# Layer 3 of a fused four-layer kernel: gate chain in a PSUM tile of its own, five padded images, block copies moved from DMA to ScalarE and GpSimd

## The chip, the cores and the metric

The kernel runs on one core of one Trainium2 chip. Its time is the device time of one execution in microseconds. The core has five engines that matter here: TensorE (PE, with its weight loads PEld), VectorE (DVE), ScalarE (ACT), GpSimd (POOL) and SyncE (SP), whose queue starts the DMAs.

## The reference

Four layers work one after the other on x of shape (4, 256, 48, 48), each on a group-normalised input and each added to x: attention with eight heads, an 11-tap gated block, non-local attention with batch norm, and layer 3, which alone the change touches (with the few lines ahead of it):

```python
xw = _gn(x)                                   # group norm, 32 groups
p = jnp.mean(xw, axis=(2, 3))
h = jax.nn.leaky_relu(p @ attn_w1.T, 0.01)    # 256 -> 64
a = jax.nn.sigmoid(h @ attn_w2.T)             # 64 -> 256
y = xw * a[:, :, None, None]
y = depthwise_conv3x3(y, refine_w, 'SAME') + refine_b
y = (y - mean_hw(y)) * rsqrt(var_hw(y) + 1e-5)
x = x + leaky_relu(y, 0.01)
```

So layer 3 gates each channel with a number that a small two-layer network makes of the channels' means (the gate chain), convolves each channel with its own 3x3 filter, and normalises each channel of each image.

## The kernel before

Channels lie on the 128 partitions, in two halves (NK = 2); an image has 2304 pixels in a row. Layer 3 works on eight tiles: four images (order 1, 2, 3, 0) times two halves. For each tile the following is done.

- **Product and grow.** `w_product` (L1444) multiplies the last step of layer 2 into PSUM, `grow` (L1497, VectorE) scales it, adds x and writes it into a padded image of 50 by 50 (`pads`, tile i uses `pads[i % 4]`). Three products and three grows make a tile; they share one PSUM buffer, `w_tile()`. `border` (L1506, L1509, GpSimd) writes the rim. `square` (L1521, ScalarE) takes the sum of squares of each third.
- **Spread.** TensorE does the depthwise convolution with small weights, 32 channels at a time, that read three column-shifted copies of the channels on different partitions. `spread_out` fills these copies (`shifted`, three buffers of half an image): eight blocks that change partition go by DMA, four that stay on their partitions by GpSimd (first half), or two by DMA and two by ScalarE (second half). `place` issues one block (L1535 to L1541).
- **Convolution.** `Conv.products` (L1662) makes one sixth of the tile in PSUM (`cv_tile()`, three buffers, each holding two sixths): 12 matmuls, which the profile shows as 24 records.
- **Statistics and end.** `evict` (L1674, ScalarE) writes each third to SBUF with its sum, `centre` (L1681) makes a rough mean of the first third, the other `square` (L1685, ScalarE) takes the squares about it, `moments`, `scales` and `shift` (L1693 to L1733, VectorE, with a root on GpSimd, L179) give scale and offset, `scale` (L1739, ScalarE) applies them, `leak` (L1745) and `gain` (L1750) on VectorE apply the leaky ReLU and add x, `store` (L1756) starts the DMA to the output. The last tile takes its statistics with `bn_stats` (L1705) from PSUM.
- **Gate chain.** For each image once, `Chain.steps`: `total` (L1580), `groups` (L1587, a matmul), `inverse` (L1591 and a root on GpSimd), `pooled`, `first_layer` (L1602), `hidden` (L1610), `second_layer` (L1615), `gate` (L1622, ScalarE) and `scaled` (L1626 to L1631). Its matmuls write columns 384 and up of the convolution's PSUM tile in use (`now["ps"]`), and ScalarE reads them out (`read`, L1575). `judge` (L1768 to L1782) takes one vote on the range of earlier sums in the same manner.

The order on every engine is fixed by hand: a list of events, each with a slot and a rank. A slot is the time of one convolution sixth, six to a tile, 48 in all (T). Within a slot the ranks run FRONT, CONV, PRODUCT, GROW, MID, EVICT, SMALL, MOMENTS, SQUARE, SCALE, LAST, PLACE, STORE, and the instructions go into the engines' queues in that order (strict order on all five). `put_tile`, `put_before` and `put_chain` say in which slot each step falls, t being the tile's first slot:

```python
at(t - 11 + c, PRODUCT, lambda c=c: product(c))
at(max(0, t - 6 + 3 * h), PLACE, lambda i=i, h=h: spread_out(i, h))
at(t + 10 + g, LAST, lambda g=g: cv.leak(g))
put_chain(max(t - 1, 0), chains[i // NK].steps(8 if i else 7))
```

Ahead of the first slot stands a stretch that ends layer 2: the last unit of attention is summed (`total_here`, L399 and L401), folded (L387), divided (L391), multiplied for the batch statistics (L1084, L1365, L1136), `note` (L407 to L410) records sums for the vote, and batch scale and offset follow (L1374 to L1387). Then the first two tiles are grown (L1497), spread by `spread_first` and squared.

Of the kernel before, what the change touches and what calls it, by code (L numbers as in the profile page):

```python
# [78 lines left out]
def usual_path(  # L79
# [315 lines left out]
    def total_here(u):  # L395

        ps = pj_tile()
        for h, c in enumerate(HALVES):
            nc.tensor.matmul(ps[c, :SL], lhsT=ones, rhs=u["acc"][:, h, :], start=True, stop=True)  # L399
        u["rinv"] = rpool.tile([P, SL], F32, tag="rinv", name="rinv")  # L400
        nc.vector.reciprocal(u["rinv"], ps[:, :SL])  # L401
        u["l"] = ps
# [24 lines left out]
    def last(u, t):  # L427

        take(u)
        if u.get("soon"):  # L430
            todo = [
                (fills, 1, lambda: total_here(u)), (due, 2, lambda: fold(u, nc.vector)),
                (due, 2, lambda: divide(u, nc.vector)),
            ]
            if u.get("final"):
                noted.append(lambda: note(u))
            else:
                todo.append((due, 2, lambda: note(u)))
# [920 lines left out]
    attend(phases)  # L1359
    for b in range(NX):  # L1360
        sample_means(b)
    last_y = [w_mul(B - 1, k, L2C - 1, wide=True) for k in range(NK)]
    for k in range(NK):
# [23 lines left out]
    nc.vector.tensor_sub(bi2, vec[:, V_WB, :], bi2)  # L1387
    noted[0]()
    strict.close()
# [37 lines left out]
    CL = CH - 2  # L1427
    pads = [lp.tile([P, W2 * W2], F32, tag=f"pad{i}", name=f"pad{i}") for i in range(4)]
    shifted = [lp.tile([P, 4, CH], F32, tag=f"sh{i}", name=f"sh{i}") for i in range(3)]

    def rows_of(i):
        return pads[i % 4].rearrange("p (r c) -> p r c", c=W2)

# [18 lines left out]
    first = [w_product(0, c, cv_tile()) for c in range(L2C)]  # L1452
    ahead = [w_product(1, 0, w_tile())]

# [14 lines left out]
    def columns_of(ps, n):  # L1469
# [4 lines left out]
        of_groups, lhsT=gmat, rhs=means.rearrange("p b k -> p (b k)"), start=True, stop=True  # L1474
    )
    gm = lp.tile([P, B, NK], F32, name="gm")
    edge = lp.tile([P, B, NK], F32, name="edge")
# [52 lines left out]
    def place(i, h, j, q, how):  # L1530
        to = shifted[(2 * i + h) % 3][32 * q : 32 * q + 32, j, :CL]
        c0 = h * HB * W2 + SHIFT[j, q]
        fr = pads[i % 4][32 * j : 32 * j + 32, c0 : c0 + CL]
        if how == "sp":
            nc.sync.dma_start(to, fr)  # L1535
        elif how == "act":
            nc.scalar.copy(to, fr)
        elif how == "pool":
            nc.gpsimd.tensor_copy(to, fr)
        else:  # L1540
            nc.vector.tensor_copy(to, fr)  # L1541
# [3 lines left out]
    def spread_out(i, h):  # L1545

        for j, q in AWAY:
            place(i, h, j, q, "sp")
        for j in range(4):
            place(i, h, j, j, ("sp", "act")[j % 2] if h else "pool")  # L1550

# [11 lines left out]
    class Chain:  # L1563
# [4 lines left out]

        def steps(self, last):
            of, b = {}, self.b  # L1570

            def read(p):
                of["raw"] = small.tile([P, NK], F32, tag="chain", name="chain")
                n = 1 if p < P else NK
                nc.scalar.copy(of["raw"][0:p, 0:n], of["ps"])  # L1575
                return of["raw"][0:p, 0:n]

# [7 lines left out]
            def groups():  # L1585
                of["ps"] = now["ps"][:, 0:NK]
                nc.tensor.matmul(of["ps"], lhsT=gmat, rhs=of["sq"], start=True, stop=True)  # L1587

            def inverse():
                gv = small.tile([P, NK], F32, tag="gn_gv", name="gn_gv")  # L1590
                nc.vector.tensor_scalar(gv, of["raw"], GN_EPS, None, ALU.add)  # L1591
                of["rs"] = small.tile([P, NK], F32, tag="gn_rs", name="gn_rs", bufs=6)
                rsqrt(of["rs"], gv)
# [5 lines left out]
            def first_layer():  # L1599
                of["ps"] = now["ps"][0:D, 0:1]  # L1600
                for k in range(NK):
                    nc.tensor.matmul(  # L1602
                        of["ps"], lhsT=w1[:, k, :], rhs=of["pm"][:, k : k + 1],
                        start=k == 0, stop=k == NK - 1,
                    )

            def hidden():
                raw = of["raw"][0:D, 0:1]
                of["hl"] = hl = small.tile([D, 1], F32, tag="hl", name="hl")
                nc.vector.scalar_tensor_tensor(hl, raw, SLOPE, raw, ALU.mult, ALU.max)  # L1610

            def second_layer():
                of["ps"] = now["ps"][:, 0:NK]
                for k in range(NK):
                    nc.tensor.matmul(  # L1615
                        of["ps"][:, k : k + 1], lhsT=w2[:, k * P : (k + 1) * P], rhs=of["hl"],
                        start=True, stop=True,
                    )
# [5 lines left out]
            def scaled():  # L1624
# [8 lines left out]
            return [  # L1633
                (0, MID, total), (1, SMALL, groups),
                (2, FRONT, lambda: read(P)), (2, MID, inverse),
                (3, MID, pooled), (4, SMALL, first_layer),
                (5, FRONT, lambda: read(D)), (5, MID, hidden), (last - 1, SMALL, second_layer),
                (last, FRONT, gate), (last, MID, scaled),
            ]

    class Conv:
# [9 lines left out]
        def products(self, s):  # L1651
            g, h = s // 2, s // L2C
            if s % 2 == 0:
                self.ps[g] = cv_tile()
            now["ps"] = self.ps[g][:, s % 2, SL:]
            out = self.ps[g][:, s % 2, :SL].rearrange("p (r c) -> p r c", c=HW)
# [105 lines left out]
    def judge():  # L1762
# [10 lines left out]
        def count():  # L1773
            of["ps"] = now["ps"][0:1, 0:1]
            nc.tensor.matmul(of["ps"], lhsT=of["okm"], rhs=ones[:, 0:1], start=True, stop=True)

        def read():
            of["n"] = lp.tile([1, 1], F32, name="votes")
            nc.scalar.copy(of["n"], of["ps"])

        def compare():
            nc.vector.tensor_scalar(sound, of["n"], P - 0.5, None, ALU.is_ge)  # L1782

        return [(0, FRONT, lows), (1, SMALL, count), (2, FRONT, read), (2, MID, compare)]

# [33 lines left out]

    now = {}  # L1820

    def put_chain(t, parts):
# [3 lines left out]
    def put_before(t, i):  # L1826
# [10 lines left out]
        at(t - 11, PLACE, lambda: border(i))  # L1837

    def put_tile(t, cv, final):
# [14 lines left out]
        for g in range(NG3):  # L1854
            at(t + 9 + (0 if soon else g), SCALE, lambda g=g: cv.scale(g))
            dt = 10 + (min(g, 1) if soon else g)
            at(t + dt, LAST, lambda g=g: cv.leak(g))
            at(t + dt, LAST, lambda g=g: cv.gain(g))
            at(t + dt + 1 - soon, STORE, lambda g=g: cv.store(g))

# [4 lines left out]
    for i, cv in enumerate(convs):  # L1865
# [12 lines left out]
    for t in range(max(T, max(events) + 1)):  # L1878
        for _, fn in sorted(events.get(t, ()), key=lambda job: job[0]):
            fn()  # L1880
        if t == T - 1:
            cv = convs[-1]
            cv.stats(NSL - 1)
            cv.aggregate()
            cv.scales()
            cv.shift()
            for g in range(NG3):
                cv.scale(g, cv.ps[g])
                cv.leak(g)
                cv.gain(g)  # L1890
                cv.store(g)
    said = nc.values_load(sound[0:1, 0:1])
# [845 lines left out]
```

## Time and profile before

| what | value |
|---|---|
| median of three runs | 3557.1 us (3553.09 to 3557.35) |
| the profiled execution | 3548.05 us |
| its span, first to last instruction | 3546.3 us |
| its mean granted TensorE clock | 0.990 |
| first convolution slot starts | 3375.0 us into the span |
| last convolution matmul ends | about 3528.1 us |
| last VectorE operation ends | about 3541.5 us |

Busy us of each engine in stretches of layer 3 (two tiles each in the first four rows, then the tail):

| stretch, us | PE | DVE | ACT | POOL | clock | DMA share |
|---|---|---|---|---|---|---|
| 3375.0 to 3414.75 | 36.3 | 12.1 | 26.3 | 19.0 | 0.87 | 0.78 |
| 3414.75 to 3456.5 | 34.6 | 30.9 | 28.4 | 18.0 | 0.88 | 0.77 |
| 3456.5 to 3497.3 | 33.8 | 27.5 | 28.1 | 16.7 | 0.92 | 0.89 |
| 3497.3 to 3528.1 | 26.7 | 18.8 | 21.0 | 7.4 | 0.94 | 0.63 |
| 3528.1 to 3546.3 | 0.0 | 11.6 | 2.8 | 0.5 | 0.60 | 0.35 |

Layer 3 with its lead-in is the last 190 us, about 5% of the span. A line of the timeline has start and length in us, the engine, the line of the kernel, output and input, the number of instructions that were merged, and in brackets the idle time before with what ended it.

### The profile page before, as it was taken

The numbers are of one execution on the slowest core, as the hardware profiler recorded it, in microseconds if no ns is written. First come the engines' busy times: TensorE is split into PE (matmuls) and PEld (weight loads), VectorE is DVE, ScalarE is ACT, GpSimd is POOL, SyncE is SP. The second block draws the span as 40 slices with busy tenths as digits, with TensorE's granted clock in tenths as the row PEclk, the third lists the DMA queues.
The fourth block names the chain that finished last, engine by engine and source line by source line (L and its number), as shares of the span: only waits on it lengthen the run. The fifth ranks groups of instructions, "written<-read, shape, count | busy, mean of one in ns | idle before, by whom it ended". The sixth has DMA issues, their size and how long they took to land. (4 is left out here: it accounts for less than half of the span.)

```text
span 3546.3 us, 88389 instructions
## 1 busy us (share of the span) xinstructions
PE 3431.1 (97%) x37036; PEld 1729.9 (49%) x37036; DVE 2547.1 (72%) x3475; ACT 2370.6 (67%) x3842; POOL 814.8 (23%) x619
## 2 busy tenths in 40 slices
PE   8999999999999999999999999999999999898886
PEld 4554555554444444444444444444444445565422
DVE  3455545567788788687887886878878879655856
ACT  4665666665886796558867976579668755565465
POOL 2333333321101010000111100110100117665442
PEclk9999999999999999999999999999999999999988
DMA  2211111111111111221111111111111100000076
GB/s 94 48 26 22 26 22 26 22 26 22 22 26 22 26 22 26 55 46 21 26 20 26 22 27 21 26 22 26 22 22 22 22 8 6 6 7 6 4 199 200
DMA packets 122423, 118.93 MB, mean 34 GB/s; under 512 B 59056, under 2 KB 112928, under 8 KB 121248
## 3 DMA queue, kind: packets, MB, share of 16 engines
q1 hardware_dynamic: 119264, 111.03, 16.7%
q8 instruction: 292, 4.78, 0.6%
q10 hardware_dynamic: 2752, 2.17, 0.2%
q14 instruction: 115, 0.94, 0.1%
HBM read 56.99 MB, written 11.80 MB: 19 GB/s over the span
## 5 line engine op out<-in xcount | busy, mean ns | idle before, releaser
L296 ACT ACTIVATE pt<-sc 128x768 f32<-128x768 f32 x1944 | 1475.3, 811 | 727.1 <-PE sc L290 717.0
L336 DVE TENSOR_TENSOR acc<-acc,pt 128x768 f32<-128x768 f32 x1368 | 1369.3, 1001 | 174.3 <-ACT pt L296 74.4
L310 PE MATMUL av<-pt,v 64*64 64x384 f32 x13824 | 1274.7, 484 | 0.0
L290 PE MATMUL sc<-q,k 64*64 64x384 f32 x13824 | 1269.9, 482 | 0.5 <-ACT pt L296 0.5
L290 PEld LDWEIGHTS sc<-q,k 64*64 64x64 f32 x13824 | 525.4, 133 | 589.5 <-issue 543.4
L310 PEld LDWEIGHTS av<-pt,v 64*64 64x64 f32 x13824 | 518.1, 133 | 598.9 <-issue 565.9
L391 POOL TENSOR_TENSOR o<-o,rinv 128x384 f32<-128x384 f32 x95 | 115.7, 1218 | 1735.8 <-DMA rinv<-rinv 1735.8
L321 POOL TENSOR_TENSOR half<-pt 128x768 f32<-128x768 f32 x189 | 364.4, 1932 | 537.9 <-ACT pt L296 499.9
L336 DVE TENSOR_TENSOR acc<-acc,half 128x768 f32<-128x768 f32 x171 | 194.1, 1135 | 229.5 <-POOL half L321 228.5
L674 DVE SCALAR_TENSOR_TENSOR x<-pj,bo,x 128x384 f32<-128x384 f32 x192 | 118.4, 617 | 311.2 <-PE pj L661 309.9
L850 ACT ACTIVATE prod<-pd,wt 128x256 f32<-128x256 f32 x486 | 337.1, 765 | 0.2
L578 PE MATMUL pj<-xs,w 128*128 128x384 f32 (+1 forms) x720 | 275.4, 505 | 0.0
L578 PEld LDWEIGHTS pj<-xs,w 128*128 128x128 f32 x720 | 124.1, 189 | 127.9 <-issue 39.5
L310 PE MATMUL av<-pt,qv 64*64 64x384 f32 x1728 | 174.5, 491 | 0.0
L290 PE MATMUL sc<-qv,kd 64*64 64x384 f32 x1728 | 171.5, 485 | 2.4 <-ACT pt L296 2.4
L873 DVE TENSOR_REDUCE prod<-prod 128x256 f32<-128x1280 f32 x114 | 168.7, 1480 | 0.3 <-ACT prod L850 0.3
L661 PE MATMUL pj<-o,wo 128*128 128x384 f32 (+1 forms) x384 | 159.8, 499 | 5.8 <-issue 3.6
L609 PEld LDWEIGHTS pj<-w,xs 128*128 128x128 f32 x1080 | 134.5, 191 | 24.1 <-issue 1.2
L387 POOL TENSOR_TENSOR o<-raw 128x384 f32<-128x384 f32 x95 | 125.2, 1318 | 43.3 <-ACT raw L383 43.3
L609 PE MATMUL pj<-w,xs 128*128 128x128 f32 x1080 | 134.9, 275 | 0.0
L330 DVE TENSOR_TENSOR acc<-pt 128x768 f32<-128x768 f32 x99 | 112.4, 1135 | 26.3 <-ACT pt L296 26.3
L1662 PE MATMUL cv<-sh,taps 96*32 96x384 f32 (+1 forms) x1152 | 111.2, 529 | 17.3 <-ACT chain L1575 9.1
(248 smaller groups left out, 2370.0 us busy)
## 6 DMA issues: line engine op xcount, KB each, us to landing
xs<-in_x_dram SPq DMA_DIRECT2D x90, 384.0 KB
sh<-pad SPq DMA_DIRECT2D x140, 162.2 KB
rinv<-rinv SPq DMA_DIRECT2D x208, 94.5 KB
out_dram<-x SPq DMA_DIRECT2D x24, 384.0 KB
l<-row SPq DMA_DIRECT2D x416, 1.5 KB
w<-in_wqkv_dram SPq DMA_DIRECT2D x32, 192.0 KB
x<-in_x_dram SPq DMA_DIRECT2D x4, 1152.0 KB
x<-in_x_dram SPq DMA_DIRECT2D x9, 384.0 KB
```

The costliest lines, as they stand in the source:

```text
L290: nc.tensor.matmul(ps[c * D : (c + 1) * D, h, :SL], lhsT=u["of"]["k"][r, j0 : j0 + D], rhs=u["of"]["q"][r, u["qc"]], start=True, stop=True,)
L296: nc.scalar.activation(pt, ps[:, :, :SL], AF.Exp, scale=u["scale"])
L310: nc.tensor.matmul(u["av"][h * D : (h + 1) * D, half, :SL], lhsT=value(u, j, h)[r], rhs=pt[r, h, :], start=j == 0, stop=j == JB - 1,)
L321: nc.gpsimd.tensor_add(half, pts[0], pts[1])
L336: nc.vector.tensor_add(u["acc"], u["acc"], term)
L387: eng.tensor_add(u["sum"], u["raw"][:, 0, :], u["raw"][:, 1, :])
L578: nc.tensor.matmul(ps[:, :n], lhsT=at["w"][:, k, t, :], rhs=xs[s][:, k, :n], start=k == 0, stop=k == NK - 1,)
L609: nc.tensor.matmul(ps[:, i * P : (i + 1) * P], lhsT=xs[s][:, k, i * P : (i + 1) * P], rhs=at["w"][:, k, 2, :], start=k == 0, stop=k == NK - 1,
L661: nc.tensor.matmul(ps[:, :n], lhsT=wo[:, p, k * P : (k + 1) * P], rhs=o["o"][:, :n], start=True, stop=True,)
L674: nc.vector.scalar_tensor_tensor(xs, ps[:, :SL], pair["bo"][:, k : k + 1], xs, ALU.add, ALU.add)
L850: nc.scalar.activation(bufs[n % 3][:, :, min(n, 1) + i].rearrange("p (r c) -> p r c", c=AS), pd[:, PAD + dr : PAD + dr + AS, PAD + dc : PA ...
L873: nc.vector.tensor_reduce(to, bufs[n % 3][:, :, : min(n, 1) + len(taps)], AX.X, ALU.add)
```

## The change

- The gate chain's and the vote's matmuls write a `w_tile()` of their own; VectorE reads `groups` and the hidden layer (with a copy first) directly, and ScalarE's `read` is gone. ScalarE still reads the gate. The chain of an image starts at slot t - 2 and is spread anew: total -2, groups -1, inverse 0, pooled 1, first layer 3, hidden 4, second layer 5, gate 6, scaled 7. The loop now runs from the earliest event, slot -2.
- Five padded images instead of four. Products, grows and squares of a tile come one slot earlier.
- `centre` is a ScalarE multiplication, behind the first `evict`.
- Blocks of the second half that stay on their partitions: three by ScalarE and one by GpSimd, none by DMA.
- In the next-to-last tile, leak, gain and store of the second and third part come behind the last tile's scales.
- Ahead of layer 3: the last unit's fold and the means of image 0 are put ahead of the reciprocal, the note comes directly behind the last products, the means of the other images around it, and the product for tile 1 comes behind the matmul over groups of the means.

```diff
@@ total_here
         u["rinv"] = rpool.tile([P, SL], F32, tag="rinv", name="rinv")
+        if u.get("final"):
+            fold(u, nc.vector)
+            sample_means(0)
         nc.vector.reciprocal(u["rinv"], ps[:, :SL])
@@ after attend(phases)
-    for b in range(NX):
+    last_y = [w_mul(B - 1, k, L2C - 1, wide=True) for k in range(NK)]
+    noted[0]()
+    for b in range(1, NX - 1):
         sample_means(b)
-    last_y = [w_mul(B - 1, k, L2C - 1, wide=True) for k in range(NK)]
...
-    noted[0]()
+    sample_means(NX - 1)
@@ layer 3
-    pads = [lp.tile([P, W2 * W2], F32, tag=f"pad{i}", name=f"pad{i}") for i in range(4)]
+    NPAD = 5
+    pads = [lp.tile([P, W2 * W2], F32, tag=f"pad{i}", name=f"pad{i}") for i in range(NPAD)]
...
     first = [w_product(0, c, cv_tile()) for c in range(L2C)]
-    ahead = [w_product(1, 0, w_tile())]
...
         of_groups, lhsT=gmat, rhs=means.rearrange("p b k -> p (b k)"), start=True, stop=True
     )
+    ahead = [w_product(1, 0, w_tile())]
@@ spread_out
-            place(i, h, j, j, ("sp", "act")[j % 2] if h else "pool")
+            place(i, h, j, j, "act" if h and j != 2 else "pool")
@@ Chain.steps
-                of["ps"] = now["ps"][:, 0:NK]
+                of["ps"] = w_tile()[:, 0, 0:NK]
                 nc.tensor.matmul(of["ps"], lhsT=gmat, rhs=of["sq"], start=True, stop=True)
...
-                nc.vector.tensor_scalar(gv, of["raw"], GN_EPS, None, ALU.add)
+                nc.vector.tensor_scalar(gv, of["ps"], GN_EPS, None, ALU.add)
...
-                raw = of["raw"][0:D, 0:1]
+                raw = small.tile([D, 1], F32, tag="hraw", name="hraw")
+                nc.vector.tensor_copy(raw, of["ps"])
...
-                (0, MID, total), (1, SMALL, groups),
-                (2, FRONT, lambda: read(P)), (2, MID, inverse),
-                (3, MID, pooled), (4, SMALL, first_layer),
-                (5, FRONT, lambda: read(D)), (5, MID, hidden), (last - 1, SMALL, second_layer),
-                (last, FRONT, gate), (last, MID, scaled),
+                (-2, MID, total), (-1, SMALL, groups), (0, FRONT, inverse),
+                (1, MID, pooled), (3, SMALL, first_layer), (4, MID, hidden),
+                (5, SMALL, second_layer), (6, FRONT, gate), (7, FRONT, scaled),
@@ Conv.centre
-            nc.vector.tensor_scalar(self.c, self.st[:, 0, 0:1], -1.0 / GW, None, ALU.mult)
+            nc.scalar.mul(self.c, self.st[:, 0, 0:1], -1.0 / GW)
@@ judge
-        return [(0, FRONT, lows), (1, SMALL, count), (2, FRONT, read), (2, MID, compare)]
+        return [(0, MID, lows), (2, SMALL, count), (3, FRONT, compare)]
@@ put_before (border likewise at t - 12)
-            at(t - 11 + c, PRODUCT, lambda c=c: product(c))
-            at(t - 11 + c, GROW, lambda c=c: grow(i, c, held[c]))
-            at(t - 10 + c, SQUARE, lambda c=c: square(i, c))
+            at(t - 12 + c, PRODUCT, lambda c=c: product(c))
+            at(t - 12 + c, GROW, lambda c=c: grow(i, c, held[c]))
+            at(t - 11 + c, SQUARE, lambda c=c: square(i, c))
@@ put_tile
-        at(t + 3, FRONT, cv.centre)
+        at(t + 2, EVICT, cv.centre)
...
+            if soon and g:
+                late.append((cv, g))
+                continue
+            at(t + 10 + g, LAST, lambda g=g: cv.leak(g))
+            at(t + 10 + g, LAST, lambda g=g: cv.gain(g))
+            at(t + 11 + g, STORE, lambda g=g: cv.store(g))
@@ the loop
-            put_chain(max(t - 1, 0), chains[i // NK].steps(8 if i else 7))
+            put_chain(t, chains[i // NK].steps())
-    put_chain(8, judge())
+    put_chain(7, judge())
...
+    for g in range(NG3):
+        cv.scale(g, cv.ps[g])
...
+    for tile, g in late + [(cv, g) for g in range(NG3)]:
+        tile.leak(g)
+        tile.gain(g)
+        tile.store(g)
```

More of the change, by code (lines that the diff above doesn't have):

```diff
@@ L431, in last @@
             todo = [
-                (fills, 1, lambda: total_here(u)), (due, 2, lambda: fold(u, nc.vector)),
-                (due, 2, lambda: divide(u, nc.vector)),
+                (fills, 1, lambda: total_here(u)), (due, 2, lambda: divide(u, nc.vector)),
             ]
@@ L437, in last @@
             else:
+                todo.insert(1, (due, 2, lambda: fold(u, nc.vector)))
                 todo.append((due, 2, lambda: note(u)))
@@ L1427, in usual_path @@
     CL = CH - 2
-    pads = [lp.tile([P, W2 * W2], F32, tag=f"pad{i}", name=f"pad{i}") for i in range(4)]
+    NPAD = 5
+    pads = [lp.tile([P, W2 * W2], F32, tag=f"pad{i}", name=f"pad{i}") for i in range(NPAD)]
     shifted = [lp.tile([P, 4, CH], F32, tag=f"sh{i}", name=f"sh{i}") for i in range(3)]
     def rows_of(i):
-        return pads[i % 4].rearrange("p (r c) -> p r c", c=W2)
+        return pads[i % NPAD].rearrange("p (r c) -> p r c", c=W2)
     def inside(i, c):
@@ L1532, in place @@
         c0 = h * HB * W2 + SHIFT[j, q]
-        fr = pads[i % 4][32 * j : 32 * j + 32, c0 : c0 + CL]
+        fr = pads[i % NPAD][32 * j : 32 * j + 32, c0 : c0 + CL]
         if how == "sp":
@@ L1567, in __init__, with steps @@
             self.n, self.b = n, SEQ[n]
-        def steps(self, last):
+        def steps(self):
             of, b = {}, self.b
[L1572 to L1576, printed above, removed]
             def total():
@@ L1599, in first_layer @@
             def first_layer():
-                of["ps"] = now["ps"][0:D, 0:1]
+                of["ps"] = w_tile()[0:D, 0, 0:1]
                 for k in range(NK):
@@ L1612, in second_layer @@
             def second_layer():
-                of["ps"] = now["ps"][:, 0:NK]
+                of["ps"] = w_tile()[:, 0, 0:NK]
                 for k in range(NK):
@@ L1654, in products @@
                 self.ps[g] = cv_tile()
-            now["ps"] = self.ps[g][:, s % 2, SL:]
             out = self.ps[g][:, s % 2, :SL].rearrange("p (r c) -> p r c", c=HW)
@@ L1773, in count @@
         def count():
-            of["ps"] = now["ps"][0:1, 0:1]
+            of["ps"] = w_tile()[0:1, 0, 0:1]
             nc.tensor.matmul(of["ps"], lhsT=of["okm"], rhs=ones[:, 0:1], start=True, stop=True)
-        def read():
-            of["n"] = lp.tile([1, 1], F32, name="votes")
-            nc.scalar.copy(of["n"], of["ps"])
         def compare():
-            nc.vector.tensor_scalar(sound, of["n"], P - 0.5, None, ALU.is_ge)
-        return [(0, FRONT, lows), (1, SMALL, count), (2, FRONT, read), (2, MID, compare)]
+            nc.vector.tensor_scalar(sound, of["ps"], P - 0.5, None, ALU.is_ge)
+        return [(0, MID, lows), (2, SMALL, count), (3, FRONT, compare)]
     chains = [Chain(n) for n in range(B)]
@@ L1818, in at @@
         events.setdefault(t, []).append((rank, fn))
-    now = {}
     def put_chain(t, parts):
@@ L1833, in put_before @@
         for c in range(L2C):
-            at(t - 11 + c, PRODUCT, lambda c=c: product(c))
-            at(t - 11 + c, GROW, lambda c=c: grow(i, c, held[c]))
-            at(t - 10 + c, SQUARE, lambda c=c: square(i, c))
-        at(t - 11, PLACE, lambda: border(i))
+            at(t - 12 + c, PRODUCT, lambda c=c: product(c))
+            at(t - 12 + c, GROW, lambda c=c: grow(i, c, held[c]))
+            at(t - 11 + c, SQUARE, lambda c=c: square(i, c))
+        at(t - 12, PLACE, lambda: border(i))
+    late = []
     def put_tile(t, cv, final):
@@ L1855, in put_tile @@
             at(t + 9 + (0 if soon else g), SCALE, lambda g=g: cv.scale(g))
[L1856 to L1859, printed above, removed]
+            if soon and g:
[4 more added lines that the diff above has]
+            at(t + 11 + g, STORE, lambda g=g: cv.store(g))
     def reload(k):
@@ L1873, in usual_path @@
         if i % NK == 0:
-            put_chain(max(t - 1, 0), chains[i // NK].steps(8 if i else 7))
+            put_chain(t, chains[i // NK].steps())
         if i < NK:
             at(t + 14, STORE, lambda k=cv.k: reload(k))
-    put_chain(8, judge())
-    for t in range(max(T, max(events) + 1)):
-        for _, fn in sorted(events.get(t, ()), key=lambda job: job[0]):
-            fn()
[L1881 to L1891, printed above, removed]
+    put_chain(7, judge())
+    for t in range(min(events), T):
+        for _, fn in sorted(events.pop(t, ()), key=lambda job: job[0]):
+            fn()
+    cv = convs[-1]
+    cv.stats(NSL - 1)
+    cv.aggregate()
+    cv.scales()
+    cv.shift()
+    for g in range(NG3):
+        cv.scale(g, cv.ps[g])
+    for t in sorted(events):
+        for _, fn in sorted(events[t], key=lambda job: job[0]):
+            fn()
+    for tile, g in late + [(cv, g) for g in range(NG3)]:
+        tile.leak(g)
+        tile.gain(g)
+        tile.store(g)
     said = nc.values_load(sound[0:1, 0:1])
```

## The prediction

> **What bounds the kernel now.** I read the page first: TensorE is busy 97% of the span, but that is the attention stage. The diff touches only the last 190 us, so I went on to the busy times by stretch from 3355 us on, and there no engine stands above 90% for long. The waits of TensorE from 3373 us to the end name what stops it:
>
> ```profile
> PE cv L1662 <- ACT chain L1575: 9.1, 4, 2.9
> PE cv L1662 <- ACT ga L1622: 6.9, 4, 3.2
> PE cv L1587 <- DVE gn_sq L1581: 5.6, 4, 3.4
> ```
>
> All are the gate chain: its small products lie in the convolution's PSUM tile, so the next slice waits until ScalarE has read them. TensorE's timeline shows what follows such a wait:
>
> ```profile
> 3375.01 8.37 PE L1662 MATMUL cv<-sh,taps 96*32 96x384 f32 x48 [1.29 <-DVE pad L1497]
> 3383.31 0.88 PE L1444 MATMUL w<-y,Ww 64*64 64x384 f32 x8
> 3384.40 0.38 PE L1587 MATMUL cv<-gn_sq,gmat 128*128 128x2 f32 x2 [0.21 <-DVE gn_sq L1581]
> ...
> 3438.44 0.60 PE L1615 MATMUL cv<-hl,w 64*128 64x1 f32 x4
> 3442.22 3.30 PE L1662 MATMUL cv<-sh,taps 96*32 96x384 f32 x24 [3.18 <-ACT ga L1622]
> 3445.45 1.35 PE L1444 MATMUL w<-y,Ww 64*64 64x384 f32 x8
> 3446.73 2.14 PE L1662 MATMUL cv<-sh,taps 96*32 96x384 f32 x24
> ```
>
> A slot (24 records) takes 2.0 us, or 3.3 after the gap. The gaps of slots 2 to 47 sum to 21.5 us and the slow slots behind them to 10 us more: 32 us is the most that the chain can give back. The stretches around this gap (busy us, clock) show why they are slow:
>
> ```profile
> 3439.65:3443.06 3.41, 0.84 (x12) 1.00 0.85 246
> 3443.06:3446.47 3.41, 3.41 (x26) 0.50 0.92 256
> 3446.47:3449.88 3.41, 3.41 (x40) 1.00 0.99 298
> ```
>
> Last, all engines in 3432 to 3475 us, to see what stands behind TensorE. VectorE's leak (L1745) and gain (L1750) take 0.95 and 1.02 alone, and 2 each while GpSimd copies:
>
> ```profile
> 3433.98 2.57 ACT L1537 COPY sh<-pad 32x1298 f32<-32x1298 f32 x2
> ...
> 3436.68 7.15 POOL L1539 COPY sh<-pad 32x1298 f32<-32x1298 f32 x4 [6.99 <-PE cv L1662]
> ...
> 3438.85 1.90 DVE L1750 SCALAR_TENSOR_TENSOR x<-pad,bi,x 128x768 f32<-128x768 f32 x1
> ...
> 3440.68 2.01 DVE L1745 SCALAR_TENSOR_TENSOR x<-x 128x768 f32<-128x768 f32 x1
> ...
> 3445.60 1.02 DVE L1750 SCALAR_TENSOR_TENSOR x<-pad,bi,x 128x768 f32<-128x768 f32 x1
> ```
>
> [...] 0.84 us of work in the window did not save the clock, while 2.18 us in 3456.7 to 3460.1 did. [...] four copies of 1.26 took 7.15, and both VectorE operations doubled.
>
> **The change, part by part.** Let tile i occupy slots 6i to 6i+5. An even tile holds a chain's reads.
>
> *Transition.* The fold (0.49) moves into VectorE's 0.97 us wait ahead of the reciprocal: -0.5. The note (1.35) moves under the last product's wait, one pair of means (0.4) into the wait for the reciprocal root (0.55): the means come 1.65 earlier, but the 24 product records ahead (4.12 us, cold) only 0.5. The product over groups now precedes the product for tile 1 (0.95), so it runs at 3367.5, not 3368.6. VectorE's grows and the first copies start 1.05 earlier.
>
> *Start of the chain.* Total and group product move from slots 0 and 1 to -2 and -1, ahead of the first slice in TensorE's queue. They need all six squares of tiles 0 and 1, which ScalarE ends at 3383.5, after five copies and six squares with no idle from 3370.68. With the 1.05 that is 3382.45; total 0.6, group product 0.4: the first slice starts at 3383.5, not 3375.0. Queued behind this wait is all of layer 3's convolution: +8.5. Back comes: slots 0 and 1 then run with ScalarE idle ahead of them, and no later stop in tiles 0 and 1 (gaps 2.9 and 0.3 there, 3.4 at the next). Stepping on: slot 0 cold 4.1 (clock back at 3388.4 by the window), product 1.0, slots of 2.0, products of 0.85, small products 0.8: tile 1 begins at +17.6. Tile 1: six slots 12, three products 2.5, group product 0.3: tile 2 at +32.4 = 3415.9, against 3414.75. Net **+1.2**; from -1.2 (warm at once) to +2.9 (another cold window).
>
> *Centre on ScalarE.* Removes ScalarE's 14.6 us of waiting for L1681 (7 times), adds about 0.15 each (L1575, a ScalarE copy as small; at worst the 0.2 of L1674's accumulator read more). *Blocks.* Per tile -2 DMAs of 18 on SP's queue, +1 ScalarE copy (1.28), +1 GpSimd copy (1.26). The DMAs hide: the spread issues within 5 us and has 6 slots; TensorE's waits name it never. If that cover were gone, 2 of 18 would still be a gain. *Products one slot earlier, fifth pad.* The leak of the slot and the next grow now share slots 0 and 1. *Reads by VectorE.* Three ScalarE reads go, but the only w buffer is now shared: the product of an even tile's slot 0 waits for VectorE's inverse, that of an odd tile for ScalarE's gate. A small VectorE read of PSUM costs 0.17 (L1483), the copy ahead of the hidden layer as much more; both are in the sums below. The vote (L1768 to L1782) comes once, under 0.7 us of VectorE in tile 1, where VectorE waits for TensorE anyway: 0; without that cover 0.7.
>
> *Steady pair of tiles.* TensorE alone needs 2 x 14.6 + 1.2 = 30.4; ScalarE 2 x (12 x 0.92 + 3 x 1.285 + 0.15) = 30.1. Neither bounds; the loop through VectorE and ScalarE does. Durations from the traced rows, start to start; leak plus gain 1.95, grow 1.15, moments and scales 1.45:
>
> - Even, from the end of gain(1): inverse and product 1.1; grow(0) 1.25; leak and gain(2) 4.4, since GpSimd's four copies are queued behind the root that waits for the inverse, and so run just then; grow(1) 1.15; pooled 0.25; moments 1.75; grow(2) 1.2. Then ScalarE: square 0.95, scale(0) 0.95, three copies 3.85, evict(1) 0.95, scale(1) 0.9. Leak and gain(1) 3.7: the odd tile's copies have begun. Sum 22.4.
> - Odd: grow(0) 1.15, leak and gain(2) 2.0, scaled 0.65, grow(1) 1.15, moments 1.45, grow(2) 1.2, ScalarE 7.6, leak and gain(1) 2.1. Sum 17.3.
>
> 39.7 a pair, against 41.75 and 40.8 (tiles 2-3, 4-5): **-3.15**. TensorE idles some 2.7 us at each tile's first product and goes cold, but has 9 us of slack in a pair. What is late next is thus VectorE's turn, not the chain's read.
>
> *Last pair and tail.* From tile 6's start the last VectorE operation came 44.2 later (3541.54). New: tile 5's shift at 13.8, held by GpSimd's copies; then ScalarE's scale, three copies, evict, scale, square, scale, gate, evict, square to 24.2. VectorE: gain(2) of tile 5 at 24.4, scaled and moments 26.9, shift 27.7, leak and gain(0) 30.7, last statistics 31.7, the last tile's scales 33.2, five pairs of leak and gain (two were deferred) 9.8, and 0.6 more lag from the pairs before: 43.6. **-0.6**, from -3 to +2.
>
> Sum +1.2 - 3.15 - 0.6 = -2.55: 3543.7 us of span, with the 1.75 us around it 3545.5 against the profiled 3548.05. That execution is 9 us under the median; I carry the difference over: 3557.1 - 2.6 = **3554.5**.
>
> **Rivals.** *Faster: the lock costs little.* If copies and two-input operations don't meet, 2.4 + 1.75 + 0.55 = 4.7 go from each pair: 35.0, and 9.4 more: 3545. For it: the four copies from 3456.67 took 5.84, not 7.15, so they met less. Against: in an even tile queue order puts the copies right behind the inverse, and the inverse right ahead of the leak.
> *Slower: the copies slide onto the moments.* The root holds the four copies until VectorE's inverse. If they end later than I put them (12.5 us into the even tile), the four two-input small operations of the moments each wait for a running copy, up to 1.26: +5.0 a pair, 44.7, which makes 3564.5. The total turns slower than before from 41.0 a pair. For it: small operations already show 1.19 instead of 0.15 beside copies (L1610). Against: two copies will have gone by then.
> *The chain was all:* 32 us back, 3525. Against: ScalarE's and VectorE's loop, and the 8.5 us start. Under 3 in 100.
>
> **Numbers.** 0.2% (7.1 us) is about what a measurement of this kernel can tell from no change. The forecast is within it. I give it 0.58; the faster cases 0.29; slower 0.13. The range 3544 to 3564 goes to both rivals and takes in start and tail bounds; the forecast's own is 3550 to 3559.
>
> **What would show it.** Right: TensorE's first slice starts near 3383.5 behind the group product; waits "w <- DVE gn_gv" and "w <- ACT ga" of some 2.7 us a tile take the place of the chain reads; pairs near 39.7; leak and gain near 2 us each beside GpSimd. Wrong: a first slice before 3380, or pairs under 37 or over 42.

## The result and the profile after

The changed kernel takes 3550.1 us (median of 20 runs, 3547.92 to 3554.32), the kernel before 3555.1 us (20 runs, 3550.31 to 3558.22) on the same chip. The ratio is 0.9988 with a 95% interval of 0.9982 to 0.9994, that is 2.1 to 6.4 us less. The forecast of -2.6 us, less than 0.2%, lies in that interval.

**A measure for the parts.** The profiled spans (3546.3 before, 3547.2 after) show no gain, for two reasons. In the profiled execution after, the attention stage ended 3.67 us later (the matmul over the last sums, L399, starts at 3358.37 instead of 3354.70), which is ahead of anything that the change touches here; and the last stretch, from the last VectorE operation to the end of the span, was 6.6 us instead of 4.8, of which it is open whether the change made it longer. So I use the **length of layer 3**: from the start of that matmul to the end of the last VectorE operation. It is 186.84 us before and 182.18 after, -4.66, which agrees with the ratio of the runs; with the 1.8 us of the last stretch it would be -2.8, and so would that. A length is read from one execution of each kernel, so its scatter isn't known: below, lengths and ratios differ by up to 2 us in most runs and by 3 in one (e12). Times after that matmul, in us:

| | before | after | difference |
|---|---|---|---|
| first ScalarE block copy starts | 15.98 | 15.06 | -0.92 |
| first convolution slot starts | 20.31 | 28.91 | +8.60 |
| tile 2 starts | 59.94 | 61.79 | +1.85 |
| tile 4 starts | 101.68 | 100.04 | -1.64 |
| tile 6 starts | 142.45 | 139.16 | -3.29 |
| last convolution matmul ends | 173.38 | 166.98 | -6.40 |
| last VectorE operation ends | 186.84 | 182.18 | -4.66 |

TensorE's waits of the kernel after, from 3373 us to the end (total, times, longest), answer to those of the prediction:

```profile
PE w L1586 <- DVE gn_sq L1580: 11.0, 1, 11.0
PE w L1449 <- DVE gn_gv L1590: 5.8, 2, 3.1
PE w L1449 <- ACT ga L1622: 4.5, 2, 2.3
```

The reads of the chain by ScalarE are gone from the head of the list. In their place stand one wait of 11.0 us at the start and four waits of the next tile's first product for the one `w` buffer, which the chain now holds. TensorE's timeline shows the first, and then one of the four with the cold slot (one at half the clock) behind it:

```profile
3374.91 0.88 PE L1449 MATMUL cv<-y,Ww 64*64 64x384 f32 x8 [0.69 <-DVE pad L1502]
3386.80 0.56 PE L1586 MATMUL w<-gn_sq,gmat 128*128 128x2 f32 x2 [11.01 <-DVE gn_sq L1580]
3387.28 4.14 PE L1659 MATMUL cv<-sh,taps 96*32 96x384 f32 x24
...
3463.61 1.38 PE L1449 MATMUL w<-y,Ww 64*64 64x384 f32 x8 [3.06 <-DVE gn_gv L1590]
3464.92 3.27 PE L1659 MATMUL cv<-sh,taps 96*32 96x384 f32 x24
```

The stretches around that gap (TensorE's busy time and records, granted clock, DMA share, GB/s) look as they did before around a chain read: a nearly empty window, then one at about half the clock.

```profile
3460.10:3463.50 3.40, 0.45 (x8) 1.00 1.02 241
3463.50:3466.90 3.40, 3.29 (x24) 0.55 1.04 327
```

VectorE and GpSimd behind the same read, from the timeline: the root waits for VectorE's read at 3463.40, four copies follow it, and leak (L1742) and gain (L1747) run beside them.

```profile
3463.70 0.71 POOL L179 TENSOR_TENSOR gn_rs<-gn_gv,mhalf 128x2 f32<-128x2 f32 x1 [9.45 <-DVE gn_gv L1590]
3464.35 6.45 POOL L1544 COPY sh<-pad 32x1298 f32<-32x1298 f32 x4
...
3466.10 1.64 DVE L1742 SCALAR_TENSOR_TENSOR x<-x 128x768 f32<-128x768 f32 x1
...
3467.77 1.90 DVE L1747 SCALAR_TENSOR_TENSOR x<-pad,bi,x 128x768 f32<-128x768 f32 x1
```

Alone, leak and gain take 0.96 and 1.02 in this trace too, and four lone copies of 1.26 would take 5.04. So leak loses 0.68 here, gain 0.88 and the copies 1.41. Lastly the piece of ScalarE's queue that the later half of each tile goes through:

```profile
3475.31 3.85 ACT L1542 COPY sh<-pad 32x1298 f32<-32x1298 f32 x3
3479.19 0.81 ACT L1671 ACTIVATE x<-cv 128x768 f32<-128x768 f32 x1
...
3480.12 1.01 ACT L1736 ACTIVATE x<-x,in_sf,in_sc 128x768 f32<-128x768 f32 x1
...
3481.16 1.93 DVE L1742 SCALAR_TENSOR_TENSOR x<-x 128x768 f32<-128x768 f32 x1 [3.71 <-ACT x L1736]
```

VectorE stands 3.71 us, waiting for a scale (L1736) that is queued behind three block copies and an evict.

### The profile page after: what moved, and what is told of

It is laid out like the page before. It is cut to its first block, busy times and chain, and to the rows that moved or that the text cites. A ratio compares the mean times of both kernels' runs of the same rounds, so it can differ in the third digit from the quotient of the medians.

```text
span 3547.2 us, 88373 instructions
## 1 busy us (share of the span) xinstructions
PE 3426.8 (97%) x37036; PEld 1727.0 (49%) x37036; DVE 2550.9 (72%) x3472; ACT 2380.1 (67%) x3847; POOL 818.5 (23%) x626
## 5 line engine op out<-in xcount | busy, mean ns | idle before, releaser
L383 ACT COPY raw<-av 128x768 f32<-128x768 f32 x108 | 86.4, 800 | 48.0 <-PE av L310 45.6
```

## The experiments

Three theories went in. **The loop** (that of the prediction): layer 3 moves at the pace of a loop through VectorE and ScalarE, so what counts is what stands in that loop, and the early first chain loses time. **The lock** (so the prediction calls what is seen above: leak, gain and the copies lose 0.68, 0.88 and 1.41 us when they run side by side): VectorE and GpSimd holding each other up, not ScalarE's queue, set that pace. **The chain**: its waits were the delay, and the other parts are along for the ride. Each run below starts from the changed kernel unless it says otherwise; ratios are to the kernel before, on the same chip, and "length" is the measure above.

**e1: only the first image's chain goes back behind the first slots.**

```diff
@@ Chain.steps
+            if self.n == 0:
+                return [
+                    (0, MID, total), (1, SMALL, groups), (2, FRONT, inverse),
+                    (2, MID, pooled), (4, SMALL, first_layer), (5, MID, hidden),
+                    (5, SMALL, second_layer), (6, FRONT, gate), (7, FRONT, scaled),
+                ]
```

> The changed kernel with the first image's gate chain put back behind the first slices (total in slot 0, group product in slot 1, inverse in slot 2; the later images as changed). The layer-3 length is counted from the start of the matmul over the last attention unit's sums to the end of the last VectorE operation; it was 186.8 us before and 182.2 after. My theory: the early chain holds the first slice for 8.6 us, and about 6 of these are lost for good, so tile 2 starts at 56 instead of 61.8, later pairs stay at 38 to 39, length 176, time about 3544. Rival: the loop through ScalarE and VectorE absorbs the early start, tile 2 at 60 to 62 as now, length 181 to 182.

Ratio 0.9970 (0.9958 to 0.9982); length 177.24, 4.9 less than the changed kernel. TensorE's timeline:

```profile
3378.32 0.81 PE L1665 MATMUL cv<-sh,taps 96*32 96x384 f32 x2 [2.00 <-DVE pad L1502]
3381.01 4.71 PE L1665 MATMUL cv<-sh,taps 96*32 96x384 f32 x22 [1.88 <-DMA sh<-pad]
...
3390.82 0.35 PE L1586 MATMUL w<-gn_sq,gmat 128*128 128x2 f32 x2 [1.36 <-DVE pad L1502]
```

The first slot starts 19.43 us after the L399 matmul (28.91 with the change), and the chain's matmul then costs 1.36 where it cost 11.01. Of the 9.5 us gained at the start, 4.8 are left at tile 2 (56.95) and 4.9 at the end. The start of the chain was a loss inside the change, as the prediction had it.

**e2: the first half's four blocks by DMA, so that GpSimd has hardly a copy left to lock with.**

```diff
-            place(i, h, j, j, "act" if h and j != 2 else "pool")
+            place(i, h, j, j, ("act" if j != 2 else "pool") if h else "sp")
```

> The changed kernel with the four same-partition blocks of the first half by DMA instead of GpSimd, so that no GpSimd copy stands beside leak, gain and the small operations (four DMAs more per tile). My theory: the lock costs some 4.7 us in each pair of tiles and about 3 in the last pair: pairs of 34 to 35, length 170, time about 3538. Rival: 20 block DMAs a tile are too many, blocks land late, TensorE waits for them, pairs stay at 38 or grow, length 182 or more.

Ratio 0.9977 (0.9968 to 0.9986); length 178.56, only 3.6 less: a length near 170 was far off. The odd tiles became 1.2 to 2.0 us shorter, the even ones (20.1 and 20.5) not at all. The timeline of the same place in an even tile shows why:

```profile
3466.90 0.88 PE L1449 MATMUL w<-y,Ww 64*64 64x384 f32 x8 [3.06 <-DVE gn_gv L1590]
3467.71 3.68 PE L1659 MATMUL cv<-sh,taps 96*32 96x384 f32 x24
...
3468.90 0.95 DVE L1742 SCALAR_TENSOR_TENSOR x<-x 128x768 f32<-128x768 f32 x1
...
3469.89 1.02 DVE L1747 SCALAR_TENSOR_TENSOR x<-pad,bi,x 128x768 f32<-128x768 f32 x1
...
3471.32 0.97 PE L1449 MATMUL w<-y,Ww 64*64 64x384 f32 x8
...
3472.37 1.14 DVE L1502 SCALAR_TENSOR_TENSOR pad<-w,sc,x 128x384 f32<-128x384 f32 x2 [1.46 <-PE w L1449]
```

Leak and gain are at their lone times again (0.95 and 1.02 us), so the lock is gone. But the 3.06 us gap is not, TensorE's next slot is cold (3.68 us), the product behind it comes at 3471.32, and VectorE waits 1.46 us for it. The cold slot took the lock's place: the two had lain side by side. The rival of this run, blocks that land late, is small beside that: TensorE's waits for block DMAs sum to 1.1 us. The lock alone does not set the pace.

**e3: the second half's blocks as in the kernel before (two ScalarE copies, two DMAs).**

```diff
-            place(i, h, j, j, "act" if h and j != 2 else "pool")
+            place(i, h, j, j, ("sp", "act")[j % 2] if h else "pool")
```

> The changed kernel with the second half's same-partition blocks as before (two by ScalarE, two by DMA). My theory: ScalarE's third copy (1.28 us) lies on the loop in every tile, so the pairs get 2.6 shorter (36 to 36.5) and length falls to about 176: this part of the change costs time. Rival: the DMAs were what the change had to get rid of; then pairs stay at 38 to 39 or grow, length 182 to 185.

Ratio 0.9963 (0.9949 to 0.9977); length 172.69, 9.5 less; pairs of tiles 35.4 and 35.7, shorter than expected. The same place in the timeline:

```profile
3477.47 2.57 ACT L1542 COPY sh<-pad 32x1298 f32<-32x1298 f32 x2
...
3482.04 1.36 DVE L1742 SCALAR_TENSOR_TENSOR x<-x 128x768 f32<-128x768 f32 x1 [2.55 <-ACT x L1736]
```

VectorE's stand is 2.55 us instead of 3.71, one copy less. Moving blocks from DMA to the engines was the costliest part of the change.

**e12: which of the two engines? One of the three ScalarE blocks goes to DMA, GpSimd keeps its own.**

```diff
-            place(i, h, j, j, "act" if h and j != 2 else "pool")
+            place(i, h, j, j, ("sp", "act", "pool", "act")[j] if h else "pool")
```

> The changed kernel with the second half's first block by DMA again, so that ScalarE makes two copies a tile (as before) while GpSimd keeps the one it was given. It tells apart which of the two moved blocks cost the 9.5 us. My theory: it is ScalarE's third copy, 1.28 us on the loop in each tile, length 173 to 174.5, pairs of 35.5 to 36.3. Rival: it is GpSimd's copy beside VectorE's small operations (the offset's scale took 0.67 instead of 0.15 there), length 179 to 182, pairs above 37.5.

Ratio 0.9971 (0.9959 to 0.9983); length 173.41, 8.8 less, pairs 35.4 and 35.6. So it is ScalarE's third copy; e3, which also takes GpSimd's copy away, is only 0.7 shorter. The groups of instructions say how many copies there are; first the kernel before, then the one after:

```profile
L1537 ACT COPY sh<-pad 32x1298 f32<-32x1298 f32 x19 | 24.2, 1273 | 16.7 <-DVE pad L1497 16.3
```

```profile
L1542 ACT COPY sh<-pad 32x1298 f32<-32x1298 f32 x26 | 33.0, 1269 | 15.8 <-DVE pad L1502 15.4
```

Seven copies more, 8.8 us more, and the length grows by as much. That the sums agree so well is partly chance. Up to tile 2 the two added copies cost 0.3 us; in each of the two pairs that follow, two copies (2.5 us) cost 2.9 and 3.5; the last one, from tile 6's start to the end, goes with 2.1. By the ratios the run is about 6 us faster than the changed kernel, with an interval wide enough for 8.8. In the loop of the pairs, then, the third copy costs at least its own length.

**e4: the centre back on VectorE.**

```diff
-            nc.scalar.mul(self.c, self.st[:, 0, 0:1], -1.0 / GW)
+            nc.vector.tensor_scalar(self.c, self.st[:, 0, 0:1], -1.0 / GW, None, ALU.mult)
...
-        at(t + 2, EVICT, cv.centre)
+        at(t + 3, FRONT, cv.centre)
```

> The changed kernel with the centre back on VectorE at the front of slot 3. My theory: the first square of a tile then waits until VectorE has done grow(2) and the shift, so it moves behind them on the loop: +1.2 to +1.5 us per tile, pairs of 41 to 42, length 188 to 190. Rival: ScalarE waits there for grow(2) anyway, pairs stay at 38 to 39.

Ratio 1.0013 (1.0004 to 1.0021): without the centre on ScalarE the change is slower than the kernel before. Length 192.54, 10.4 more, and pairs of 42.9 and 42.1, more than expected. ScalarE's waits name it (total, times, longest); first the kernel before, then this run:

```profile
ACT junk L1685 <- DVE in_c L1681: 14.6, 7, 2.7
```

```profile
ACT junk L1682 <- DVE in_c L1678: 20.7, 7, 6.8
```

Why it grew by 6.1 was not tried. In e9 (below), which has the new chain with the old blocks, it is 18.1 us, so over half of the growth is there with the chain alone; the rest could be the longer leak and gain ahead of it in VectorE's queue.

**e10: the kernel before, with the centre alone on ScalarE** (e4's edit the other way round).

> The kernel before with the centre alone moved to ScalarE, behind the first evict. My theory: each tile's first square no longer waits for VectorE, so scale(0) and all behind it come 1.3 us earlier in a tile: pairs of 38 to 39.5 instead of 41.7 and 40.8, length 178 to 181. Rival: TensorE's waits for the chain's reads bound the kernel before, pairs stay within 0.5 and length at 185.5 to 187.

Ratio 0.9974 (0.9965 to 0.9983); length 177.71, 9.1 less than before. This one instruction gives about twice what the whole change gives. Its waits of TensorE, against 9.1, 6.9 and 5.6 in the kernel before:

```profile
PE cv L1662 <- ACT chain L1575: 7.2, 4, 2.4
PE cv L1662 <- ACT ga L1622: 4.2, 4, 1.9
PE cv L1587 <- DVE gn_sq L1581: 3.0, 3, 2.0
```

Even the chain's waits shrink, by 7.2 in all, with no line of the chain touched. My reading is that ScalarE comes to its reads earlier when it no longer stands for the centre ahead of them.

**e9: the chain alone** (own tile, reads by VectorE, new slots, five pads, products one slot earlier; centre, blocks, lead-in and end as before).

> Of the change only the gate chain (own PSUM tile, VectorE's reads, new slots) with the fifth padded image and the products one slot earlier; centre, blocks, the stretch ahead and the end as before. If the parts add up, the length is 182.2 + 10.4 (centre) - 9.5 (blocks) + 0.6 (stretch ahead) + 1.4 (end) = 185.1 against 186.8 before: the chain's reads, 32 us of gaps and slow slots, were worth 2 us. Rival: the chain is the gain and the centre only saves its place in this order, length 176 to 180.

Ratio 0.9991 (0.9984 to 0.9997); length 183.30, 3.5 less than before, and 1.8 shorter than the 185.1 that the single parts added up to. Taken alone, then, the chain was not the delay that its waits suggest. Since the loss of 4.9 by the early first chain (e1) is in it, the chain's own tile with what goes with it (five pads, earlier products) is worth some 8.4. From the other side, e10 to e8 (below) is 9.4 less, 2.0 of which are lead-in and deferral: 7.4. What this bundle owes to the tile, to the reads by VectorE, to the pads and to the earlier products was not taken apart.

**e7: VectorE's and ScalarE's reads of the chain earlier in their queues, so that the `w` buffer comes free sooner.**

```diff
-                (-2, MID, total), (-1, SMALL, groups), (0, FRONT, inverse),
+                (-2, MID, total), (-1, SMALL, groups), (-1, MOMENTS, inverse),
...
-                (5, SMALL, second_layer), (6, FRONT, gate), (7, FRONT, scaled),
+                (5, SMALL, second_layer), (5, MOMENTS, gate), (7, FRONT, scaled),
```

> The changed kernel with the two reads that hold the w buffer put earlier in their engines' queues: the inverse directly behind the group product (ahead of leak and gain of slot 5), the gate directly behind the second layer (ahead of slot 5's square and scale). It tests whether TensorE's gaps of 2.2 to 3.1 us at a tile's first product are what the change now loses. My theory: TensorE's gaps go or fall under 1 us, but VectorE still has leak and gain of slot 5 ahead of the first grow, and GpSimd's copies start earlier and meet these instead, so that pairs shorten only by 1.5 to 2 (36.5 to 37.5), length 178 to 179.5. Rival 1: the gaps are on the path, pairs shorten by their sum, 4 to 5 us (34), length 172 to 174. Rival 2: nothing, 182.

Ratio 0.9981 (0.9975 to 0.9988); length 178.27, 3.9 less. TensorE's waits:

```profile
PE w L1586 <- DVE gn_sq L1580: 11.0, 1, 11.0
PE w L1449 <- DVE pad L1502: 9.1, 4, 2.6
...
PE w L1449 <- ACT ga L1622: 0.8, 2, 0.4
```

The waits for `gn_gv` are gone and those for `ga` fell from 4.5 to 0.8, but 9.1 us of waits for VectorE's grow came up: of 9.5 us of waits taken away, 3.9 came through.

**e5 and e6: the lead-in, and the deferral in the next-to-last tile, each undone.** The lead-in has fold, note, means and the product for tile 1 in the old order; for e6:

```diff
-            if soon and g:
-                late.append((cv, g))
-                continue
-            at(t + 10 + g, LAST, lambda g=g: cv.leak(g))
-            at(t + 10 + g, LAST, lambda g=g: cv.gain(g))
-            at(t + 11 + g, STORE, lambda g=g: cv.store(g))
+            dt = 10 + (min(g, 1) if soon else g)
+            at(t + dt, LAST, lambda g=g: cv.leak(g))
+            at(t + dt, LAST, lambda g=g: cv.gain(g))
+            at(t + dt + 1 - soon, STORE, lambda g=g: cv.store(g))
```

> The changed kernel with the stretch ahead of layer 3 as before (fold, means, note and the product for tile 1 in their old places). My theory: every later mark comes 0.9 us later, nothing else moves: layer-3 length 183.1 against 182.2. Rival: it is all hidden behind other waits, 182.2.

> The changed kernel with leak, gain and store of the next-to-last tile's second and third part back in their old slots ahead of the last statistics. My theory: the last statistics then wait for two pairs of leak and gain (3.9 us) while VectorE's work after them shrinks by as much, and ScalarE's scale (about 1 us) is no longer covered: length 183.2. Rival: VectorE is late in any case and the order among its own jobs is worth nothing, 182.2.

Lead-in: ratio 0.9991 (0.9983 to 0.9999), first copies 0.92 later, length 182.78 (+0.6). Deferral: ratio 0.9992 (0.9984 to 1.0000), length 183.56 (+1.4). The lengths give a sign; the ratios can't be told from that of the changed kernel.

**e8: e1 and e3 together. e11: e1, e3 and e7 together.**

> The changed kernel with both repairs: the first image's chain behind the first slices, and the second half's blocks as before (two by ScalarE, two by DMA). If the two losses are independent, as I hold, their gains add: 182.2 - 4.9 - 9.5 = 167.8 of length, about 3537 of time. Rival: both free the same slack in ScalarE's queue, length 171 to 173.

> The changed kernel with all three repairs: first chain behind the first slices, second half's blocks as before, and the two reads that hold the w buffer early in their queues. With the first two the length was 168.3, pairs 35.4 and 36.4, and TensorE had 5.7 us left to wait for inverse and gate, but also 4.5 for block DMAs. My theory: 2 of the 5.7 come back, length 166 to 167, the rest goes to the DMAs and to VectorE. Rival: the DMA engines bound it by now (their share was 1.00 in tiles 4 and 5), length 168 to 169.

e8: ratio 0.9950 (0.9936 to 0.9963), length 168.34, 13.8 less than the changed kernel where the parts add up to 14.4. e11: ratio **0.9940 (0.9926 to 0.9954)**, length 166.72, the shortest of all, 20.1 less than the kernel before and 15.5 less than the changed one; by ratio the two can't be told apart. What limits them is new; here e8's stretches of tiles 2-3 and 4-5 (busy us of PE, PEld, DVE, ACT, POOL, clock, DMA share, GB/s) and one of its waits of TensorE:

```profile
3416.60:3453.00 36.40, 31.76 (x364) 11.15 (x353) 25.63 (x55) 29.05 (x51) 17.05 (x15) 1.00 0.85 238
3453.00:3489.40 36.40, 31.61 (x351) 11.47 (x352) 26.30 (x54) 28.39 (x50) 17.02 (x15) 1.00 1.00 279
```

```profile
PE cv L1665 <- DMA sh<-pad: 4.5, 4, 2.0
```

The clock is at full speed in both stretches. The DMA share reaches 1.00 in the second, but of the 4.5 us of waits for blocks 2.6 come at the very first slot (in e1, too, 1.9), 0.7 in tile 4 and 1.2 in tile 7. So in the steady pairs blocks on DMA hardly cost anything yet, and what sets the pace of e8 and e11 is not shown.

## Why the prediction was right, step by step

**The ledger.** From the single runs, by length: the centre -9.1 (e10), the chain's own tile -8.4 (e9 without e1's part), the early first chain +4.9 (e1), the blocks +9.5 (e3; 8.8 by ScalarE's third copy, e12), the lead-in -0.6 (e5), the deferral -1.4 (e6). The sum is -5.1; the whole change measured -4.66. The terms lean on each other by 1 to 2 us: the centre is 10.4 when taken out of the changed kernel (e4), the chain 7.4 from the other side. A small net, then, of two large gains and two large losses.

**Start of the chain: right.** First slot +8.5 forecast, +8.6 measured; tile 0 17.6 against 17.95 and tile 1 14.8 against 14.93. The net at tile 2 was +1.2 and came out +1.85, 0.65 more. So the wait ahead of the first slot and its length were foreseen. With e1 the net splits: without the early chain tile 2 starts 3.0 earlier than before, and the early chain costs 4.8. The lead-in's -1.05 at the first copies came as -0.92.

**The steady pairs: right in kind, the gain too small.** The two pairs took 38.25 and 39.12, together -5.1 against the forecast -3.15. The errors of the forecast's three parts, +0.65, -2.0 and (below) -0.8, cancel in part, and that much of its agreement is luck. Here are the steps of the loop in tiles 4 and 5 from the trace (from the end of gain(1) to the end of the next):

| step | even: forecast | measured | odd: forecast | measured |
|---|---|---|---|---|
| inverse and product | 1.1 | 1.64 | | |
| grow(0) | 1.25 | 1.06 | 1.15 | 1.06 |
| leak and gain(2) | 4.4 | 3.50 | 2.0 | 1.91 |
| scaled | | | 0.65 | 0.67 |
| grow(1) | 1.15 | 1.05 | 1.15 | 1.05 |
| pooled, moments | 2.0 | 1.57 | 1.45 | 1.77 |
| grow(2) | 1.2 | 1.06 | 1.2 | 1.06 |
| ScalarE, square to scale(1) | 7.6 | 7.88 | 7.6 | 7.89 |
| leak and gain(1) | 3.7 | 3.79 | 2.1 | 1.93 |
| sum | 22.4 | 21.55 | 17.3 | 17.34 |

The one term off by much is "leak and gain(2) 4.4": VectorE's leak came 0.43 us into the second copy and took 1.64 us where the forecast had about 2, so that with the gain (1.90) the two took 3.50, start to start. In turn the product came 0.5 late, being cold (1.38 instead of 0.88). What is left is about 0.1 a grow. Tiles 2 and 3, which came out shorter still, are alike in this: leak and gain(2) took 2.9 there, with another 0.6 of waiting for the product behind the cold slot.

**Last pair and tail: right in sign.** -0.6 forecast, -1.4 measured (43.0 from tile 6's start against 44.4).

**"TensorE goes cold, but has 9 us of slack": right only in part.** In tile 4 of the changed kernel nothing waits for the cold slot, because VectorE's leak and gain, 3.50 us beside the copies, end later than the product behind it; in tile 2, where only the gain met a copy, VectorE waited 0.58 us for the product behind it. In e2 the lock is gone and the cold slot costs VectorE 1.46 us. The slack of 9 us is a sum over a pair, and it doesn't lie where the loop needs it. So the rival *the lock costs little* promised too much with 4.7 a pair: e2 took away all copies of the first half and gained 1.1 and 1.8 a pair. *The chain was all* (32 us) was rightly held unlikely: it would have been off by a factor of about four. A gap that the profile books on one wait is worth only what the next-latest wait leaves of it.

**"The DMAs hide": right** (with two DMAs a tile back, in e3, TensorE's list names one wait for blocks, of 1.4 us), and what the prediction didn't draw from it. If the DMAs cost nothing, the two copies that replace them must be costed at what they add, and ScalarE's stands in the loop: 1.28 a tile for seven tiles, 9 us (measured: 8.8 by length). The sum had it ("three copies 3.85") but never beside 2.57, so the text doesn't show that this part alone loses more than the chain gains. Likewise the centre was told as a wait of 14.6 removed and then vanished in the pair's sum: e10 shows that it was worth as much as the chain or more, 9.1 us with those 14.6 gone.

**The slower rival, *copies onto the moments*,** did not come in tiles 4 and 5 (the small operations take 0.14 to 0.32 there, and one 0.67), hardly in tile 2 (one of 0.83, one of 0.68), but it did once, in tile 6, where the four copies still ran when the moments were due. The timeline of GpSimd and VectorE there:

```profile
3503.82 5.68 POOL L1544 COPY sh<-pad 32x1298 f32<-32x1298 f32 x4
...
3504.28 1.22 DVE L1596 TENSOR_TENSOR pm<-dev,gn_rs 128x2 f32<-128x2 f32 x1
...
3505.60 1.22 DVE L1691 TENSOR_SCALAR in_mv<-in_mv 128x2 f32<-128x2 f32 x1
...
3507.05 1.11 DVE L1695 SCALAR_TENSOR_TENSOR in_ve<-in_d 128x1 f32<-128x1 f32 x1
...
3510.23 1.23 DVE L1730 TENSOR_TENSOR in_sf<-in_off,in_ri 128x1 f32<-128x1 f32 x1
```

These four operations took 0.14 to 0.24 us in tile 4 and 1.11 to 1.23 here, and ScalarE waited 5.40 us for the scale that they make; in e2, without those copies, no such wait was longer than 3.4.

**Open.** Why the chain alone (e9) gained 1.8 more than the parts add up to, and how much of the 1.8 us by which the stretch after the last VectorE operation grew belongs to the change: no run was made for either. That stretch is 4.6 to 5.1 us in the profiles of the kernel before, e4, e9 and e10, and 6.2 to 7.0 in the ten others, which is no clear sign of one part. Which piece of the chain's bundle gives its gain, and what limits e8 and e11, is open too.

## What to carry to other kernels

When two engines hand work back and forth in a strict order, find the loop and step through it: in the steady pairs here a copy moved into it cost at least its 1.28 us each time round, an instruction moved out of it gave back 9.1 us where its waits had summed to 14.6, and blocks on the DMA queue outside it cost almost nothing (in e8's steady pairs TensorE waited 0.7 us for them). Don't take the top line of the waits for the size of the prize: the chain's gaps and the slow slots behind them summed to 32 us, but taking the chain out gave 7.4 to 8.4, while a 128x1 multiplication that stood nowhere in TensorE's list (in ScalarE's it was the second line) gave 9.1 and shrank the chain's waits as well. A change of many parts should be run part by part: two of these lost what the others won.

## What the runs showed of the hardware

- In the traces of the two kernels every change of the granted clock lies on a grid of 3.41 us, and how much TensorE worked in one window of that grid goes with the clock of the next. From the L399 matmul to the last matmul the two traces have 76 windows at full clock: all 11 with up to 1.25 us of recorded TensorE work were followed by one at half the clock, all 63 with 1.92 us or more by one at full clock, and of the two between, that with 1.74 us held and that with 1.81 dropped. Coming back took more: of 23 windows at half the clock the nine with up to 2.18 us were followed by another, the 12 with 3.41 us by a full one; one with 2.83 came back and one with 3.16 didn't.
- Beside GpSimd's copies (1.26 us alone) small VectorE operations took longer too: up to 1.23 us for 128x1 (L1730) in tile 6, and among them a TENSOR_SCALAR with one tensor as input (L1691, above: 1.22, against 0.17 to 0.24 in the six other tiles, where no block copy ran beside it). Why this one was longer is not shown. A pair of grows (L1502), each with one input in PSUM, took 1.13 to 1.14 in tile 4 beside the copies, and 1.14 in e2 without them.
- A multiplication of 128x1 by ScalarE took 0.20 us (L1678 of the kernel after: 7 of them, 203 to 205 ns), where the prediction took 0.15, the time of a small ScalarE copy (L1575 of the kernel before: 149 ns in the median).
